# Two attention layers on small graphs: sums over keys by VectorE transposes and row sums, their inverses passed through DRAM

## The chip, the cores and the metric

One Trainium2 chip, one of its cores. The core has TensorE (PE: matmuls, with a weight load ahead of each; PEld), VectorE (DVE), ScalarE (ACT), GpSimd (POOL) and SyncE (SP), which here issues nearly all DMA transfers. Each engine takes its instructions in order, and an instruction may wait for semaphores that other engines or landed transfers raise. The metric is the device time of one execution in microseconds; less is better.

## What is computed

Sixty-four graphs of 256 nodes with 512 features go through two layers, each a LayerNorm, a ReLU, multi-head attention restricted by the graph's adjacency, and a residual sum. Layer 0 has 4 heads of 64 and no self-loops added (a row without neighbours becomes uniform); layer 1 has 8 heads of 64, a gamma and beta, and self-loops. All is fp32.

```python
h = relu(layernorm(x))                        # per node
q, k, v = h @ Wq, h @ Wk, h @ Wv              # split into heads of 64
sim = where(adj, (q @ k.T) / 8, -big)         # per graph and head, 256 x 256
x = x + softmax(sim) @ v @ Wo + bo            # layer 0, 4 heads

h = relu(layernorm(x))
q, k, v = split((h * gamma + beta) @ w_qkv.T)
sim = where(adj | eye, (q @ k.T) / 8, -1e9)
x = x + softmax(sim) @ v @ w_out.T + b_out    # layer 1, 8 heads
```

The softmax's divisor, the sum of the exponentials over the keys, is what the change is about. The kernel holds scores as (keys on partitions) x (queries), so the sum over keys is a sum across partitions.

## The kernel before

**Steps and places.** Two graphs make a step, and there are 32 steps. The program for PE, DVE, ACT and POOL is one list of events, each with a place in time units (`at(period, place, ...)`), sorted by place and emitted in that order; a period is 6.4 units. So for these four engines the order of the work is written by hand. SP's order is not: the framework's scheduler decides in which order SP issues the transfers.

**Heads in pairs.** Two heads (128 columns) make a pair: layer 0 has pairs 0 and 1 (`L0`), layer 1 pairs 0 to 3, taken as `L1A` = (0, 2) and `L1B` = (1, 3).

**Visits.** A period has three visits (`visit`, L1073), each for two pairs: at place 2.0 (here called X: it ends layer 0 of step s+1 and begins `L1A` of step s), at 4.5 (Q: ends `L1A`, begins `L1B`), and at 6.2 (Z: ends `L1B` of s, begins layer 0 of s+2). At its head PE runs, for the two pairs begun at the visit before, `key_sums` (L1007: the sums over keys, four groups of 32 output rows, one for each graph and head, by a matmul with ones) and `weigh` (L976: exponentials times values), and then `scores` for the two new pairs (L920). DVE adds the mask (L944), ACT takes the exponentials (L949), and POOL adds the two halves of the keys into `pd` (`key_halves`, L953), a tile with two buffers.

**Between visits** PE runs sets of seven products (Strassen's scheme, `SET`, `SETC`, `SETC0`), one product taking 1/7 unit: projections to queries and keys (`project_qk`, L803), values (`project_v1`, L844; `project_v0`, L830), output projections (`combine`, L860). The result of each product is moved out of PSUM by DVE or ACT (`evacuate`, `accumulate`), placed at the end of the product. Four PSUM banks (`m0` to `m3`) go round; PE can't write one before its last contents are out. The scheme needs sums of blocks of the activations: `act_sums0` and `act_sums1` (L409 to L414, POOL). After X come the values of step s (set at 2.0), layer 0's output projection of step s+1 (at 3.0, `SETC0`: products 1, 6, 5, 2, 7, 3, 4; product 6 multiplies block 4, which L412 writes) and the second half of the queries and keys (3.5). The output projection is added into `xt`, the residual rows.

**The inverses.** `invert` (L1022) takes reciprocals of the sums, 32 equal rows for each graph and head, from PSUM (L1029), folds an overflow check into `extremes` (L1032), and copies the rows, 32 partitions at a time, with eight transfers a pair (L1041) to all the partitions that hold the head's outputs (`invb`). `normalise` (L1046, POOL) multiplies.

**Other work that the change moves.** For step s+2: `norm0` (statistics, L576/L577), `scale_row` (L592, ACT), `turn_blocks` (L686, DVE transposes of 32x32 blocks) and `move_blocks` (L698, sixteen transfers that complete the transpose of the activations); `neighbours` (L511, DVE: whether a node has a neighbour), `neighbours_out` (L518: writes that to DRAM as `row`, 4 bytes at a time), `neighbours_in` (L523: reads it back to all partitions as `ne`). For step s+1: `load_x` (L493, loads `xt`, at X + 0.1) and `first_bias` (L498, POOL, adds a bias to `xt`, four times, at 2.5, 2.51, 2.85 and 2.86). On POOL the order after X is `key_halves`, `normalise`, `key_halves`, L498 twice, `normalise`, L409 to L414, L498 twice, and then the masks (L560, L563). The finished rows are stored by L894.

Of the kernel before, what the change touches and what calls it, by code (L numbers as in the profile page):

```python
# [315 lines left out]
def fast_path(  # L316
# [63 lines left out]
    ones = const.tile([P, 32], FP, name="ones")  # L380
    nc.vector.memset(ones, 1.0)
# [521 lines left out]
    def scores(s, lyr, pr, second):  # L903
# [32 lines left out]
        pd = sm.tile([P, 2, G, N], FP, name="pd", bufs=2)  # L936
        st["sc", lyr, pr], st["p", lyr, pr] = sc, (p, pd)

    def mask_scores(s, lyr, pr, g):

        st = S[s]
        sc, (p, pd), neg = st["sc", lyr, pr][g], st["p", lyr, pr], st[f"n{lyr}"]
        for e in range(2):
            nc.vector.tensor_tensor(p[e][:, g], sc[e], neg[:, :, g, :], ALU.add)  # L944

    def exponentials(s, lyr, pr, g):
        p, pd = S[s]["p", lyr, pr]
        for e in range(2):
            nc.scalar.activation(p[e][:, g], p[e][:, g], AF.Exp, scale=SCALE)  # L949

    def key_halves(s, lyr, pr, e):
        p, pd = S[s]["p", lyr, pr]
        nc.gpsimd.tensor_tensor(pd[:, e], p[e][:, :, 0, :], p[e][:, :, 1, :], ALU.add)  # L953


    def place_values(s, lyr):
        st = S[s]
        tile_o = act.tile([P, NB, HP1, N], FP, name="oT")
        if lyr:
            st["oT1"] = tile_o  # L960
            st["invb"] = [tile_o[:, 3], tile_o[:, 4]]
            st["inv"] = [tile_o[:, 6, i] for i in range(2)]
        else:
# [3 lines left out]
            st["inv"] = [flat[:, 12 + i] for i in range(2)]  # L967

    def weigh(s, lyr, pr):
        st = S[s]  # L970
        p, _ = st["p", lyr, pr]
# [24 lines left out]
    def key_sums(s, lyr, prs):  # L996

        st = S[s]
        bank = mm_tile([P, 2, N])
        sums_bank[:] = [banks[-1]] if len(prs) > 1 else []  # L1000
        for i, pr in enumerate(prs):
            _, pd = st["p", lyr, pr]
            st["sums", lyr, pr] = bank[:, i]
            for g in range(G):
                for e in range(2):
                    r0 = 32 * (2 * g + e)
                    nc.tensor.matmul(  # L1007
                        bank[r0:r0 + 32, i, :], ones, pd[:, e, g, :], start=True, stop=True,
                        skip_group_check=True,
                    )  # L1010

    def inverse_places(s, lyr, pr, i):

        if (s, lyr) != (NSTEP - 1, 1):
            return S[s]["inv"][i], S[s]["invb"][i]
        if pr == 0:
            invb = wqk0[:, 6].rearrange("p c k o -> p (c k o)").rearrange("p (g n) -> p g n", g=G)
        else:
            invb = act.tile([P, G, N], FP, name="invb", tag=("n0", "ne", "ab")[pr - 1])
        return bo_b[:, i * N:(i + 1) * N], invb  # L1020

    def invert(s, lyr, pr, i, halves=(0, 1)):  # L1022
        st = S[s]
        sums = st["sums", lyr, pr]
        if 0 in halves:
            st["place", lyr, pr] = inverse_places(s, lyr, pr, i)
        inv, invb = st["place", lyr, pr]
        for k in halves:
            nc.vector.reciprocal(inv[:, k * P:(k + 1) * P], sums[:, k * P:(k + 1) * P])  # L1029
        if 1 not in halves:  # L1030
            return
        nc.vector.tensor_tensor_reduce(  # L1032
            out=sums, in0=sums, in1=inv, scale=1.0, scalar=0.0, op0=ALU.add, op1=ALU.max,
            accum_out=extremes[:, units[0]:units[0] + 1],
        )
        units[0] += 1
        for g in range(G):
            for e in range(2):
                r0 = 32 * (2 * g + e)
                for d0 in range(e * DH, (e + 1) * DH, 32):  # L1040
                    nc.sync.dma_start(invb[d0:d0 + 32, g, :], inv[r0:r0 + 32, :])  # L1041
        st["invb", lyr, pr] = invb
# [30 lines left out]
    def visit(period, w, prev, cur):  # L1073
# [4 lines left out]
        if prs:  # L1078
            at(period, w, key_sums, s, lyr, prs)
            if prs[0] == 0 and not last:  # L1080
                at(period, w, place_values, s, lyr)
            for i, pr in enumerate(prs):
                k = i if len(prs) > 1 else pr % 2
                at(period, w + 0.1 * last, invert, s, lyr, pr, k, (0,) if i and not last else (0, 1))
                if not last:
                    at(period, w, weigh_out, s, lyr, pr)
                    at(period, w + (0.55 if len(prs) == 1 else (0.3, 0.75)[i]), normalise, s, lyr, pr)
        for i, pr in enumerate(cur[2]):
# [4 lines left out]
            if i == 1 and len(prs) > 1 and not last:  # L1093
                at(period, w, invert, s, lyr, prs[1], 1, (1,))
# [3 lines left out]
            for e, place in enumerate((0.23, 0.3) if one else ((0.1, 0.11), (0.35, 0.36))[i]):  # L1098
                at(period, w + place, key_halves, *unit, e)

# [24 lines left out]
    visit(-1, 1.54, none, (1, 0, (1,)))  # L1125
    for s in range(NSTEP):
# [6 lines left out]
        for t in range(NT):  # L1133
            at(p, 0.5 + 0.4 * t if s != 1 else 1.95 + 0.1395 * t, norm0, s, t)
            if s == 0:
                at(p, 0.95 + 0.4 * t, first_scale, t)
            else:
                at(p, 2.35 + 0.001 * t if s != 1 else 2.6 + 0.1 * t, scale_row, s, t)
            if not by_tensor(s, 0):
                at(p, (2.45, 2.48, 2.58, 2.6)[t], turn_blocks, s, 0, t)  # L1140
        if not by_tensor(s, 0):
            at(p, 2.61, move_blocks, s)
        for g in range(G):
            at(p, (1.8, 2.7)[s] if s < 2 else 0.7 + 0.14 * g, neighbours, s, g)
# [3 lines left out]
        else:  # L1148
            at(p, 0.9, neighbours_out, s)
            at(p, 1.9, neighbours_in, s)  # L1150
# [104 lines left out]
def kernel(tc, *args):  # L1255
# [3 lines left out]
    with tc.tile_pool(name="guard", bufs=1) as guard:  # L1259
        extremes = guard.tile([P, B // 2 * 6], FP, name="extremes")  # L1260
# [44 lines left out]
```

## Time and profile before

| | |
|---|---|
| runs | 3223.42, 3223.45, 3221.77 us; median 3223.42 |
| profiled execution | 3224.29 us, its span 3222.4 us |
| granted TensorE clock, mean | 0.999 |
| L803, all projections to queries, keys | 1186.4 us busy on PE |
| L860, output projections | 587.9 us |
| L976, exponentials times values | 352.1 us |
| L1029, reciprocals | 376 of 939 ns, 8 of 925 ns |
| L1032, check | 192 of 433 ns, each with a read of 142 ns |
| L686, transposes 128x512 | 240 of 671 ns (median) |
| L511, reductions 128x512 | 64 of 664 ns |
| transfers, median issue to landing | `row` 9.2 us, `ne` 5.1, `xt` 5.8, L1041 1.9, L698 2.0 |

A line of a timeline gives start (us from the span's start), length, engine, line, operation, output and input tile, and how many instructions are merged; brackets at its end give the idle time before it and what ended it. A line of the page's groups gives shapes, the count, then busy time and mean ns of one. SPq is SP's DMA queue; its lines show the issue of a transfer, not its flight. In a table by stretches a column is the engine's busy time with the number of instructions, and the last three are granted clock, DMA share and GB/s.

### The profile page before, as it was taken

Reading aid. Unit: us, or ns where it says so; the run is one execution under the profiler, and the core shown is the slowest. Engines: PE = TensorE matmul, PEld = TensorE weight load, DVE = VectorE, ACT = ScalarE, POOL = GpSimd, SP = SyncE. Lnnn points to the kernel's source line nnn. Section 1 sums busy time; section 2 is a strip of 40 time slices with the busy share of each in tenths; the row PEclk is TensorE's granted clock in tenths of the full one; section 3 lists DMA queues with packets and bytes.
Section 4 is the critical chain, followed back from the end, with each engine's and each line's share of the span. In section 5 each row is a group of like instructions: output and inputs, shape, how many; then the busy total and the mean of one; then the engine's idle time right before and its main releaser. Section 6 shows DMA issues by size and latency. Waiting matters only on the chain.

```text
span 3222.4 us, 59733 instructions
## 1 busy us (share of the span) xinstructions
PE 3196.6 (99%) x22002; PEld 2613.9 (81%) x22002; DVE 2091.9 (65%) x3680; ACT 1256.4 (39%) x2226; POOL 2240.0 (70%) x2124
## 2 busy tenths in 40 slices
PE   8999999999999999999999999999999999999999
PEld 6788888888888888888888888888888888888787
DVE  6656666666666666675666666666666667566655
ACT  4434343343433334343434334343433434343431
POOL 7776776677767767667677667776776766767753
PEclk9999999999999999999999999999999999999999
DMA  4132232232322322223223223232232222322311
GB/s 149 43 86 76 57 86 65 81 82 54 86 69 75 89 61 72 76 70 86 77 56 86 65 81 83 54 85 69 75 88 62 71 76 69 87 77 54 87 30 48
DMA packets 214217, 237.04 MB, mean 74 GB/s; under 512 B 75032, under 2 KB 128416, under 8 KB 213920
## 3 DMA queue, kind: packets, MB, share of 16 engines
q1 hardware_dynamic: 213488, 232.76, 26.4%
q8 instruction: 177, 2.90, 0.4%
q14 instruction: 120, 0.98, 0.2%
q10 hardware_dynamic: 432, 0.40, 0.0%
HBM read 86.12 MB, written 33.62 MB: 37 GB/s over the span
## 4 chain that ended last, share of the span: by engine, by line
PE 93%; DMA 2%; POOL 2%; SPq 1%; issue 1%; DVE 1%; POOLq 0%; DVEq 0%
PE mm L803 36%; PE mm L860 17%; PE mm L844 10%; PE sc L976 10%; PE sc L920 8%; PE mm L830 7%; PE mm L1007 3%; PE mm L920 2%; SPq L1041 1%; DMA xt<-in_x_dram 1%; POOL xt L498 1%; PE mm L886 0%; DMA h<-in_x_dram 0%; DVE oT L1029 0%; PE mm L549 0%
## 5 line engine op out<-in xcount | busy, mean ns | idle before, releaser
L803 PE MATMUL mm<-hT,wqkv 128*128 128x256 f32 x3584 | 787.5, 380 | 0.0
L803 PEld LDWEIGHTS mm<-hT,wqkv 128*128 128x128 f32 x3584 | 678.2, 190 | 102.4 <-issue 11.4
L953 POOL TENSOR_TENSOR pd<-p 128x512 f32<-128x512 f32 x383 | 479.7, 1274 | 298.3 <-ACT p L949 297.6
L860 PE MATMUL mm<-wo,oT 128*128 128x256 f32 x2632 | 587.9, 381 | 9.1 <-POOL oT L412 5.8
L860 PEld LDWEIGHTS mm<-wo,oT 128*128 128x128 f32 x2632 | 498.2, 190 | 89.0 <-issue 7.7
L1029 DVE RECIPROCAL oT<-mm 128x128 f32<-128x128 f32 x376 | 345.3, 939 | 244.3 <-PE mm L1007 239.1
L949 ACT ACTIVATE p<-p 128x512 f32<-128x512 f32 x766 | 439.6, 625 | 137.9 <-DVE p L944 137.9
L944 DVE TENSOR_TENSOR p<-sc,n 128x512 f32<-128x512 f32 x579 | 363.5, 683 | 113.7 <-PE sc L920 112.3
L844 PE MATMUL mm<-wqkv,hT 128*128 128x256 f32 x1792 | 401.9, 382 | 0.0
L803 PE MATMUL mm<-hT,wqk 128*128 128x256 f32 x1792 | 398.9, 382 | 0.8 <-DVE qk L743 0.6
L803 PEld LDWEIGHTS mm<-hT,wqk 128*128 128x128 f32 x1792 | 338.2, 191 | 56.8 <-issue 11.2
L844 PEld LDWEIGHTS mm<-wqkv,hT 128*128 128x128 f32 x1792 | 335.5, 190 | 53.7 <-issue 10.7
L976 PE MATMUL sc<-p,v 128*32 128x256 f32 x6128 | 350.2, 379 | 1.3 <-issue 1.3
L976 PEld LDWEIGHTS sc<-p,v 128*32 128x32 f32 x6128 | 199.8, 110 | 133.3 <-issue 2.3
L988 ACT COPY oT<-sc 128x512 f32<-128x512 f32 x188 | 109.3, 581 | 501.1 <-PE sc L976 495.7
L1046 POOL TENSOR_TENSOR oT<-oT 128x512 f32<-128x512 f32 x188 | 239.9, 1276 | 87.1 <-DMA oT<-oT 79.5
L920 PE MATMUL sc<-qk 64*128 64x256 f32 x2320 | 292.9, 385 | 0.0
L920 PEld LDWEIGHTS sc<-qk 64*128 64x128 f32 x2320 | 218.9, 186 | 58.9 <-issue 39.6
L771 POOL TENSOR_TENSOR xt<-xt,u 128x512 f32<-128x512 f32 x183 | 228.9, 1271 | 3.9 <-DVE xt L760 1.5
L830 PE MATMUL mm<-wv,hT 128*128 128x256 f32 x1024 | 227.0, 379 | 0.4 <-DVE qk L747 0.4
L830 PEld LDWEIGHTS mm<-wv,hT 128*128 128x128 f32 x1024 | 194.3, 190 | 27.2 <-DVE qk L747 0.7
L592 ACT ACTIVATE h<-h,mr,r 128x512 f32<-128x512 f32 x252 | 184.6, 804 | 0.0
(139 smaller groups left out, 3780.4 us busy)
## 6 DMA issues: line engine op xcount, KB each, us to landing
h<-blocks SPq DMA_DIRECT2D x960, 64.0 KB, 2.0
oT<-oT SPq DMA_DIRECT2D x1504, 32.0 KB, 1.9
xt<-in_x_dram SPq DMA_DIRECT2D x31, 1024.0 KB, 5.8
h<-in_x_dram SPq DMA_DIRECT2D x31, 1024.0 KB, 5.4
out_dram<-xt SPq DMA_DIRECT2D x31, 1024.0 KB, 4.6
ne<-row SPq DMA_DIRECT2D x30, 256.0 KB, 5.1
ad<-in_adj_dram SPq DMA_DIRECT2D x32, 128.0 KB, 9.1
wr<-in_L_gnn_w_qkv_dram SPq DMA_DIRECT2D x3, 1024.0 KB, 6.1
```

The lines of the kernel that those rows point to most:

```text
L771: (nc.vector if last else nc.gpsimd).tensor_tensor(r, r, u, ALU.add)
L803: nc.tensor.matmul(bank[:, k, :], w[:, wa, c, k, a * P:(a + 1) * P], st["hT"][:, ba, c, :], start=first and (k, c) == (0, 0), stop=(k, c) ...
L830: nc.tensor.matmul(bank, st["hT"][:, b0 + t // NIC * step, c % HC, i:i + P], wv0[:, c, :], start=(c == 0), stop=(c == NC - 1),)
L844: nc.tensor.matmul(bank[:, t, :], st["hT"][:, ba, c, t * P:(t + 1) * P], wqkv1[:, wa, c, 2, :], start=first and (t, c) == (0, 0), stop=(t, ...
L860: nc.tensor.matmul(bank[:, t, :], oT[:, ba, c, t * P:(t + 1) * P], w[:, wa, c, :], start=first and (t, c) == (0, 0), stop=(t, c) == (NIC - ...
L920: nc.tensor.matmul(sc[g][e][:, kc, :], qk[rows, 1, k0:k0 + P], qk[rows, 0, g * N:(g + 1) * N], start=True, stop=True,)
L944: nc.vector.tensor_tensor(p[e][:, g], sc[e], neg[:, :, g, :], ALU.add)
L949: nc.scalar.activation(p[e][:, g], p[e][:, g], AF.Exp, scale=SCALE)
L953: nc.gpsimd.tensor_tensor(pd[:, e], p[e][:, :, 0, :], p[e][:, :, 1, :], ALU.add)
L976: nc.tensor.matmul(po[r0:r0 + 32, g, :], st[f"v{lyr}"][:, g * NIC + kc, pr * P + r0:pr * P + r0 + 32], p[r0 // DH][:, g, kc, :], start=(kc ...
L1029: nc.vector.reciprocal(inv[:, k * P:(k + 1) * P], sums[:, k * P:(k + 1) * P])
L1046: nc.gpsimd.tensor_tensor(dst, dst, invb, ALU.mult)
```

## The change

The sums over keys no longer run on PE as matmuls with ones. For each pair, DVE transposes `pd` in 32x32 blocks (`turn_keys`: 128x1024) and reduces each block's rows (`key_quarters`: 128x1024 to 128x32); this leaves, for each query, four partial sums, one from each quarter of the partitions. One matmul a visit (`quarters`, a 128x32 matrix of four stacked identities, against `part`, 64 columns for two pairs) adds the four. The result is a 64x32 tile: one reciprocal, one check, one transfer to DRAM (`line`), and from there two transfers a pair that read the 512 values of a head back to its 64 partitions. `pd`, `turned_p`, `part` and `inv` have one buffer each. The transposes and reductions stand one at a time between evacuations; `key_halves` of the second pair move a little later at Q and Z. `norm0`, `scale_row`, `turn_blocks`, `move_blocks`, `neighbours`, `neighbours_out` and `neighbours_in` get new places.

```diff
-    ones = const.tile([P, 32], FP, name="ones")
-    nc.vector.memset(ones, 1.0)
+    quarters = const.tile([P, 32], FP, name="quarters")
+    nc.vector.tensor_tensor(quarters, ident[:, 0:32], ident[:, 32:64], ALU.add)
+    for k in (2, 3):
+        nc.vector.tensor_tensor(quarters, quarters, ident[:, 32 * k:32 * (k + 1)], ALU.add)
...
     def key_halves(s, lyr, pr, e):
-        p, pd = S[s]["p", lyr, pr]
-        nc.gpsimd.tensor_tensor(pd[:, e], p[e][:, :, 0, :], p[e][:, :, 1, :], ALU.add)
+        st = S[s]
+        p = st["p", lyr, pr]
+        if e == 0:
+            st["pd"] = sm.tile([P, 2, G, N], FP, name="pd", bufs=1)
+        nc.gpsimd.tensor_tensor(st["pd"][:, e], p[e][:, :, 0, :], p[e][:, :, 1, :], ALU.add)
+
+    def turn_keys(s):
+        st = S[s]
+        st["turned_p"] = sm.tile([P, 32, 32], FP, name="turned_p", bufs=1)
+        nc.vector.transpose(st["turned_p"], st.pop("pd").rearrange("p e g (b k) -> p (e g b) k", k=32))
+
+    def key_quarters(s, lyr, prs, i):
+        st = S[s]
+        if i == 0:
+            st["part", lyr, prs] = stat.tile([P, 2, 32], FP, name="part", bufs=1)
+        nc.vector.tensor_reduce(
+            st["part", lyr, prs][:, i], st.pop("turned_p"), axis=mybir.AxisListType.X, op=ALU.add
+        )
...
     def key_sums(s, lyr, prs):
...
-            for g in range(G):
-                for e in range(2):
-                    r0 = 32 * (2 * g + e)
-                    nc.tensor.matmul(
-                        bank[r0:r0 + 32, i, :], ones, pd[:, e, g, :], start=True, stop=True,
-                        skip_group_check=True,
-                    )
...
+        part = st.pop(("part", lyr, prs))
+        rows = 32 * len(prs)
+        bank = mm_tile([P, 32])
...
+        sums = bank[:rows]
+        nc.tensor.matmul(
+            sums, part[:, :len(prs)].rearrange("p i b -> p (i b)"), quarters, start=True, stop=True
+        )
+        inv = stat.tile([P, 32], FP, name="inv", bufs=1)[:rows]
+        nc.vector.reciprocal(inv, sums)
         nc.vector.tensor_tensor_reduce(
             out=sums, in0=sums, in1=inv, scale=1.0, scalar=0.0, op0=ALU.add, op1=ALU.max,
-            accum_out=extremes[:, units[0]:units[0] + 1],
+            accum_out=extremes[:rows, units[0]:units[0] + 1],
         )
         units[0] += 1
-        for g in range(G):
-            for e in range(2):
-                r0 = 32 * (2 * g + e)
-                for d0 in range(e * DH, (e + 1) * DH, 32):
-                    nc.sync.dma_start(invb[d0:d0 + 32, g, :], inv[r0:r0 + 32, :])
-        st["invb", lyr, pr] = invb
+        line = dram.tile([len(prs), 2, T], FP, name="line")
+        nc.sync.dma_start(line.rearrange("i e (b q) -> (i e b) q", q=32), inv)
+        for i, pr in enumerate(prs):
+            invb = inverse_place(s, lyr, pr, i if len(prs) > 1 else pr % 2)
             for e in range(2):
+                nc.sync.dma_start(
+                    invb[e * DH:(e + 1) * DH].rearrange("p g n -> p (g n)"),
+                    bass.AP(tensor=line.tensor, offset=line[i, e, 0:1].offset, ap=[[0, DH], [1, T]]),
+                )
+            st["invb", lyr, pr] = invb
...
-            for e, place in enumerate((0.23, 0.3) if one else ((0.1, 0.11), (0.35, 0.36))[i]):
+            for e, place in enumerate((0.23, 0.3) if one else ((0.1, 0.11), (0.495, 0.496) if z else (0.435, 0.436) if q else (0.35, 0.36))[i]):
                 at(period, w + place, key_halves, *unit, e)
+            if cur[:2] == (1, 0):
+                turn, add, key = 0.112, 0.113, (*cur[:2], (0, 1), pr)
+            else:
+                turn, add = (
+                    (0.31, 0.311) if one else ((0.49, 0.491), (0.63, 0.92))[i] if z else
+                    ((0.43, 0.431), (1.02, 1.021))[i] if q else ((0.29, 0.291), (0.43, 0.72))[i]
+                )
+                key = (*cur, i)
+            at(period, w + turn, turn_keys, cur[0])
+            at(period, w + add, key_quarters, *key)
...
-            at(p, 0.5 + 0.4 * t if s != 1 else 1.95 + 0.1395 * t, norm0, s, t)
+            at(p, (0.5 + 0.4 * t, 1.95 + 0.1395 * t)[s] if s < 2 else (0.95, 1.05, 1.2, 1.35)[t], norm0, s, t)
...
-                at(p, 2.35 + 0.001 * t if s != 1 else 2.6 + 0.1 * t, scale_row, s, t)
+                at(p, 1.6 + 0.001 * t if s != 1 else 2.6 + 0.1 * t, scale_row, s, t)
             if not by_tensor(s, 0):
-                at(p, (2.45, 2.48, 2.58, 2.6)[t], turn_blocks, s, 0, t)
+                at(p, AT_X - 0.00035 + 0.00001 * t, turn_blocks, s, 0, t)
         if not by_tensor(s, 0):
-            at(p, 2.61, move_blocks, s)
+            at(p, AT_X - 0.00031, move_blocks, s)
         for g in range(G):
-            at(p, (1.8, 2.7)[s] if s < 2 else 0.7 + 0.14 * g, neighbours, s, g)
+            at(p, (1.8, 2.7)[s] if s < 2 else 1.5 + 0.1 * g, neighbours, s, g)
...
-            at(p, 0.9, neighbours_out, s)
-            at(p, 1.9, neighbours_in, s)
+            at(p, 1.65, neighbours_out, s)
+            at(p, 2.6, neighbours_in, s)
```

## The prediction

> **What bounds the kernel now.** I read the page's busy times, then its chain, then the timeline of one step on TensorE (PE), on the DMA queue (SPq) and on GpSimd (POOL).
>
> ```profile
> PE 3196.6 (99%) x22002; PEld 2613.9 (81%) x22002; DVE 2091.9 (65%) x3680; ACT 1256.4 (39%) x2226; POOL 2240.0 (70%) x2124
> ...
> PE 93%; DMA 2%; POOL 2%; SPq 1%; issue 1%; DVE 1%; POOLq 0%; DVEq 0%
> ...
> L1007 PE MATMUL mm<-pd,ones 128*32 128x256 f32 x1536 | 103.0, 385 | 0.0
> ```
>
> PE is the path: every microsecond taken from it, or put on it as a wait, is a microsecond of the span. The sums over keys (L1007) are on it. One visit:
>
> ```profile
> 1635.31 1.07 PE L1007 MATMUL mm<-pd,ones 128*32 128x256 f32 x16
> 1636.20 3.64 PE L976 MATMUL sc<-p,v 128*32 128x256 f32 x64
> ```
>
> From the first L1007 to the first L976 are 0.89 us. Now the queue of SP and what hangs on it, in the step whose X visit begins at 1596.02 (0.89 us before its first L976, at 1596.91); the next X visit begins at 1695.09.
>
> ```profile
> 1599.05 6.72 SPq L1041 DMA_DIRECT2D oT<-oT  x8
> 1605.82 0.58 SPq L493 DMA_DIRECT2D xt<-in_x_dram  x1
> 1606.50 5.58 SPq L1041 DMA_DIRECT2D oT<-oT  x8
> 1612.74 10.00 SPq L698 DMA_DIRECT2D h<-blocks  x16
> ...
> 1680.96 0.37 SPq L518 DMA_DIRECT2D row<-any_of  x1
> 1681.44 1.91 SPq L485 DMA_DIRECT2D ad<-in_adj_dram  x1
> 1690.05 0.34 SPq L523 DMA_DIRECT2D ne<-row  x1
> ```
>
> ```profile
> 1611.69 2.50 POOL L498 TENSOR_TENSOR xt<-xt,bo_b 128x512 f32<-128x512 f32 x2 [0.56 <-DMA xt<-in_x_dram]
> 1614.15 1.26 POOL L1046 TENSOR_TENSOR oT<-oT 128x512 f32<-128x512 f32 x1
> 1615.37 0.73 POOL L409 TENSOR_TENSOR oT<-oT 128x256 f32<-128x256 f32 x1
> 1616.17 0.72 POOL L412 TENSOR_TENSOR oT<-oT 128x256 f32<-128x256 f32 x1
> ```
>
> ```profile
> 1616.83 6.46 PE L860 MATMUL mm<-wo,oT 128*128 128x256 f32 x28
> ```
>
> This is the stretch that decides. The load of `xt` (L493) is issued at 1605.82, 9.8 us into the visit; GpSimd waits for it by 0.56 us and then does L498 twice, L1046, L409, L412. L412 writes the block that the second product of the layer-0 output projection (L860) multiplies. That product begins four matmuls after 1616.83, at 1617.70; L412 ended at 1616.89. The slack is 0.8 us. SP issues in order: it stood before L523 until the `row` write of 1680.96 had landed (1690.05). Once, early in the span, GpSimd was late:
>
> ```profile
> 128.49 7.32 PE L860 MATMUL mm<-wo,oT 128*128 128x256 f32 x24 [5.51 <-POOL oT L412]
> ```
>
> ```profile
> 123.00:128.40 5.40, 0.00 (x0) 0.00 (x0) 0.00 (x0) 0.58 (x1) 5.40 (x7) 1.00 0.43 102
> 128.40:131.80 3.40, 3.31 (x8) 2.68 (x9) 0.69 (x1) 0.00 (x0) 3.40 (x5) 0.50 0.08 19
> ```
>
> PE stood 5.51 us, and the granted clock (the third figure from the right) was 0.50 for the 3.4 us after it.
>
> **Part 1, PE.** Ninety-five visits with two pairs lose 16 L1007 instructions, 0.888 us from first to next group, and get one fp32 matmul: two instructions with their own weights of 64 columns, 32 columns streamed. No row has that. Below: 0.28 us, two steps of 0.14 (L466: 64 matmuls, each behind a new weight load, 9.2 us). Above: 0.62, twice the 0.31 us that PE takes from the last matmul of one array shape to the first of the next. I take 0.39: a step of 0.16 (0.027 streamed, an eighth of the 0.216 per 256 columns; a load of 0.11 as in L1007; 0.025 from load to matmul), then 0.23 to leave the shape (0.027, the 0.093 by which such a change exceeds 0.216, a load of 0.11). Gain: 95 x (0.888 - 0.39) = 47 us, ends 25 and 58. The two single-pair visits give nothing.
>
> The Trainium skill (TensorE: Matmul & The Clock Gate, LDWEIGHTS) gives columns / 1.2 ns for a weight load, 53 ns for 64 columns; the rows here show 110 ns for 32 columns and 190 for 128. By the page the two loads would cost 0.11 us less a visit and the sum would be 10 us lower.
>
> **Part 2, VectorE.** A visit loses four L1029 at 0.94 and two L1032 pairs at 0.57 (4.9 us). It gets two transposes and two reductions of 128x1024: at most twice L686's 0.67 and twice L511's 0.66, so 5.3; one reciprocal, at most 0.94, and one L1032, at most 0.57. At most 1.9 us more a visit, 181 us against 1130 us of idle VectorE: hidden. The order could expose it. The first transposes stand behind the 2nd evacuation of a set (the 3rd at Q), and the second one waits for GpSimd's `pd`, which now has one buffer and so waits for the first. Walking X and Z (evacuations 0.6 apart, L953 2.5 a pair, 1.74 a product), the 4th VectorE-bound bank of Z comes free just as PE wants it: 0 to 0.2 us, 30 times, at most 6 us. I take 0. If that cover is gone, each late evacuation is PE time one for one.
>
> **Part 3, the inverses.** Reciprocals end about 1 us into a visit rather than 3 to 10. Sixteen DMAs of 0.59 us issue become one write and four reads. For Q and Z this is earlier than needed.
>
> **Part 4, the moved steps.** This is where I put the price. `turn_blocks`/`move_blocks` come forward to the head of the X visit, `neighbours` back to 1.5, `neighbours_out` to 1.65. SP's order is not written by hand, and as built it runs in every step: `row` write, `ad` load, `ne` read, `line` write of X, store, four `line` reads, sixteen moves, and only then the `xt` load. So the 16 moves (all their issues) stand before L493, and the `ne` read, which waits for `row`, before the `line` write. Microseconds from the start of X:
>
> - `row` is issued behind the second L511, which now follows the evacuation L758: that starts 5.08 before X (1690.01 to 1695.09), its successor 0.61 later, L511 takes 0.65. So -3.8. It lands 9.2 later (median of L518): 5.4.
> - `ne` 0.34; the `line` write 1.9 as L1041's landings: 7.65. Farther rows are 1.7 (a store of 128 KB) and 9.2 (`row`).
> - four reads at 0.59 issue, as L1041 (0.34 as L523 below): 10.0.
> - sixteen moves at 0.626 (10.0 by the row above): 20.05. Their transposes are long done.
> - `xt` lands 5.87 later, as 1605.82 to 1611.69: 25.9.
> - L498 twice, L1046, L409, L412, 1611.69 to 1616.89: 5.2, so 31.1.
> - PE wants it at 1617.70 - 1596.02 - 0.50 (part 1) = 21.2.
>
> So PE waits 9.9 us, in the 29 steps whose `xt` load stands there: 288 us. What is late next: after it L498's second pair ends near 35, when PE's next evacuation needs it, and the bias, masks and statistics follow at their old distances. Ends: 8.3 (`row` 8.8, reads 0.34) and 14 (`row` 11.3, a read landing as late as `ne`, 5.1, and holding the moves, which share its semaphores).
>
> The restart is not free: after the one wait of 5.51 us the 24 matmuls took 7.16 us to the next set against 5.22 at 0.2177 each, 1.94 more. 29 x 1.94 = 56 us; ends 0 (clock kept) and 3.4 a time (two such windows).
>
> The Trainium skill (DMA: Bandwidth & Descriptors, Specifications) says that pieces under 512 B cost a read-modify-write; `line` is written in pieces of 128 B. The trace has 9.2 us for pieces of 4 B and 1.9 for 1 KB; were it to cost as `row` does, the sum would be 29 x 7.3 = 212 us higher.
>
> **Sum**, against the profiled run of 3224.3 us (span 3222.4 with 1.9 around it; median of the runs 3223.4): 3224.3 - 47 + 288 + 56 = 3521.
>
> **Rivals.**
> - *The wait for `row` is not in the way* (it lands sooner, or the statistics run earlier). Then `line` lands at 0.9 + 1.9 = 2.8, reads to 5.2, moves to 15.2, `xt` at 21.1, L412 at 26.3: 5.1 us a step. 3224.3 - 47 + 148 + 56 = 3381. For it: only one DMA decides. Against: SP's waits list 243 us before L523 for `row`, 29 times.
> - *Faster: the `xt` chain is off the path.* It decides at `xt` landed by 16.0 (21.2 - 5.2). Then only part 1 counts: 3224.3 - 47 = 3177. For it: PE is 99% busy, the removal is real. Against: ten microseconds of moves now stand before the load that had 0.8 us of slack.
> - *VectorE's new order holds PE as well*, 1 us at X and Z each: 29 x 2 = 58, so 3579. For it: the transpose waits for GpSimd with evacuations behind it. Against: at X the larger wait swallows it, and VectorE idles a third of the time.
>
> **How the numbers follow.** Forecast 0.72, first rival 0.16, second 0.05, third 0.07. The forecast's own ends: 3224.3 - 58 + 29 x 8.3 = 3407 and 3224.3 - 25 + 29 x (14 + 3.4) = 3704; all bad ends together are unlikely, so I stop at 3640, and go down to 3370 for the first rival. 0.2% (6.4 us) is about what this measurement tells from no change: faster 0.05, within it 0.01, slower 0.94.
>
> **What would show it.** PE idle before L860's later products (in the changed file `combine`), released by GpSimd's activation sums, some 10 us a step; GpSimd idle before the first bias for `xt`; SP waiting for `row` across the start of X; granted clock 0.5 in short windows after each wait; from the first key-sum matmul to the first weighting matmul 0.4 us, not 0.89. I am wrong if `xt` lands by 16 us after the start of X, or if the output projection waits for nothing.

## The result, and the profile after

The changed kernel takes 3622.93 us (median of 4 runs, 3621.27 to 3624.66), the kernel before 3222.68 us beside it: a ratio of 1.1242, 95% interval [1.1223, 1.1262]. It is 400 us slower. The forecast was 3521 us within 3370 to 3640. The profiled execution took 3621.27 us, its span 3619.4.

From the page of the changed kernel: busy times, the chain by engine, and two groups.

```profile
PE 3240.9 (90%) x20660; PEld 2640.5 (73%) x20660; DVE 2152.5 (59%) x3590; ACT 1253.7 (35%) x2226; POOL 2237.7 (62%) x2124
...
PE 73%; DMA 8%; issue 7%; POOL 6%; SPq 3%; DVE 1%; ACT 0%; another core or an unknown queue 0%; POOLq 0%; DVEq 0%; ACTq 0%
...
L501 POOL TENSOR_TENSOR xt<-xt,bo_b 128x512 f32<-128x512 f32 x124 | 153.9, 1263 | 304.4 <-DMA xt<-in_x_dram 304.4
```

PE has 1342 instructions fewer (22,002 - 1536 + 194 = 20,660), and yet is busy 44.3 us longer; and it stands for 3619.4 - 3240.9 = 378.5 us, where it stood for 25.8 us before. GpSimd's bias (L501, before L498) waited 304 us for `xt`. What PE waited for, from its view of waits (total, times, longest, in us):

```profile
PE mm L863 <- POOL oT L415: 315.7, 30, 12.0
PE mm L847 <- DVE v L746: 22.9, 22, 2.3
PE sc L923 <- ACT oT L1006: 12.9, 7, 3.4
```

The first line is the wait that was forecast: product 6 of layer 0's output projection (L863, before L860) for the activation sum of block 4 (L415, before L412). One step, from the timelines. The X visit begins at 1795.22.

PE:

```profile
1795.22 0.30 PE L1022 MATMUL mm<-quarters,part 128*64 128x32 f32 x2
1795.45 3.66 PE L994 MATMUL sc<-p,v 128*32 128x256 f32 x64
...
1828.36 8.13 PE L863 MATMUL mm<-wo,oT 128*128 128x256 f32 x24 [10.81 <-POOL oT L415]
```

SP's queue:

```profile
1791.46 0.37 SPq L521 DMA_DIRECT2D row<-any_of  x1
1791.87 0.51 SPq L488 DMA_DIRECT2D ad<-in_adj_dram  x1
1800.93 0.34 SPq L526 DMA_DIRECT2D ne<-row  x1
1801.37 0.48 SPq L1033 DMA_DIRECT2D line<-inv  x1
1801.95 0.53 SPq L897 DMA_DIRECT2D out_dram<-xt  x1
1805.16 2.37 SPq L1037 DMA_DIRECT2D oT<-line  x4
1807.63 10.05 SPq L701 DMA_DIRECT2D h<-blocks  x16
1817.72 0.58 SPq L496 DMA_DIRECT2D xt<-in_x_dram  x1
```

GpSimd:

```profile
1809.05 1.28 POOL L1053 TENSOR_TENSOR oT<-oT 128x512 f32<-128x512 f32 x1 [3.71 <-DMA oT<-line]
...
1823.12 2.48 POOL L501 TENSOR_TENSOR xt<-xt,bo_b 128x512 f32<-128x512 f32 x2 [10.34 <-DMA xt<-in_x_dram]
...
1827.58 0.72 POOL L415 TENSOR_TENSOR oT<-oT 128x256 f32<-128x256 f32 x1
```

Read from SP: the `ne` read is issued only at 1800.93, when the `row` write of 1791.46 has landed; behind it stand `line`, four reads, sixteen moves, and last the load of `xt`, 22.5 us into the visit (9.8 before the change). It lands at 1823.12; L415 ends at 1828.30, and PE goes on at 1828.36. Had the load of `xt` landed 10.8 us sooner, that line of PE would carry no bracket.

The table by stretches (start:end and length, then busy us of PE, PEld, DVE, ACT, POOL, then granted clock, DMA share, GB/s) shows the clock around this wait. PE stops at 1817.55; the clock is halved from 1819.66, in the midst of the wait, until 1833.31, 4.95 us after PE goes on:

```profile
1816.24:1819.65 3.41, 1.31 (x7) 0.80 (x5) 0.81 (x2) 0.58 (x1) 0.00 (x0) 1.00 0.47 108
1819.66:1823.07 3.41, 0.00 (x0) 0.00 (x0) 0.00 (x0) 0.00 (x0) 0.00 (x0) 0.50 0.73 276
1828.36:1833.31 4.95, 4.95 (x12) 3.96 (x13) 1.38 (x2) 0.00 (x0) 4.79 (x5) 0.50 0.00 0
1833.32:1836.70 3.38, 3.37 (x16) 2.69 (x15) 2.25 (x4) 0.00 (x0) 3.38 (x3) 1.00 0.02 5
```

The account of the span, +397 us. The 22.9 us at L847 belong to the stall: that wait comes earlier in the same set, and PE goes on behind product 6 when L415 ends, however long it stood before.

| term | forecast | found | how |
|---|---|---|---|
| sums off PE | -47 | -62.5 | 95 x (0.888 - 0.23); 0.23 from 1795.22 to 1795.45 |
| stall behind X | +288 | +332.8 | 315.7 + 22.9 - 5.8 before; 30 steps of 11.3 |
| clock | +56 | +106.8 | PE busy +44.3, less the -62.5 |
| PE's other waits | 0 | +19.9 | idle +352.7 (378.5 - 25.8) less 332.8 |
| sum | +297 | +397.0 | |

### The profile page after: what moved, and what is told of

It reads as the page before. It is cut to its first block, busy times and chain, and to the rows that moved or that the text cites. A ratio compares the mean times of both kernels' runs of the same rounds, so it can differ in the third digit from the quotient of the medians.

```text
span 3619.4 us, 54427 instructions
## 1 busy us (share of the span) xinstructions
PE 3240.9 (90%) x20660; PEld 2640.5 (73%) x20660; DVE 2152.5 (59%) x3590; ACT 1253.7 (35%) x2226; POOL 2237.7 (62%) x2124
## 4 chain that ended last, share of the span: by engine, by line
PE 73%; DMA 8%; issue 7%; POOL 6%; SPq 3%; DVE 1%; ACT 0%; another core or an unknown queue 0%; POOLq 0%; DVEq 0%; ACTq 0%
PE mm L806 32%; PE mm L863 15%; PE sc L994 8%; PE sc L923 6%; PE mm L833 6%; SPq L701 3%; DMA row<-any_of 2%; PE mm L847 2%; DMA line<-inv 2%; PE mm L923 2%; POOL xt L501 2%; DMA xt<-in_x_dram 2%; DMA oT<-line 2%; POOL pd L958 2%; POOL oT L1053 1%
## 5 line engine op out<-in xcount | busy, mean ns | idle before, releaser
L863 PE MATMUL mm<-wo,oT 128*128 128x256 f32 x2632 | 669.2, 415 | 316.3 <-POOL oT L415 315.7
L863 PEld LDWEIGHTS mm<-wo,oT 128*128 128x128 f32 x2632 | 548.1, 211 | 428.7 <-POOL oT L415 328.9
L847 PE MATMUL mm<-wqkv,hT 128*128 128x256 f32 x1792 | 410.8, 385 | 23.1 <-DVE v L746 22.9
L847 PEld LDWEIGHTS mm<-wqkv,hT 128*128 128x128 f32 x1792 | 334.6, 191 | 85.6 <-DVE v L746 32.9
L501 POOL TENSOR_TENSOR xt<-xt,bo_b 128x512 f32<-128x512 f32 x124 | 153.9, 1263 | 304.4 <-DMA xt<-in_x_dram 304.4
L923 PE MATMUL sc<-qk 64*128 64x256 f32 x2320 | 309.3, 389 | 13.5 <-ACT oT L1006 12.9
L964 DVE STREAM_TRANSPOSE turned_p<-pd 128x1024 f32<-128x1024 f32 x192 | 237.4, 1237 | 109.6 <-POOL pd L958 109.6
L923 PEld LDWEIGHTS sc<-qk 64*128 64x128 f32 x2320 | 228.3, 188 | 77.8 <-issue 40.6
L761 DVE TENSOR_TENSOR u<-mm,u 128x512 f32<-128x512 f32 x62 | 42.8, 691 | 401.3 <-PE mm L863 401.3
L994 PEld LDWEIGHTS sc<-p,v 128*32 128x32 f32 x6128 | 190.3, 110 | 118.2 <-issue 0.3
L740 ACT COPY qk<-mm 128x512 f32<-128x512 f32 x96 | 55.6, 579 | 601.6 <-PE mm L806 598.2
L971 DVE TENSOR_REDUCE part<-turned_p 128x32 f32<-128x1024 f32 x192 | 232.8, 1213 | 4.4
```

Source lines behind the costliest of these rows:

```text
L847: nc.tensor.matmul(bank[:, t, :], st["hT"][:, ba, c, t * P:(t + 1) * P], wqkv1[:, wa, c, 2, :], start=first and (t, c) == (0, 0), stop=(t, ...
L863: nc.tensor.matmul(bank[:, t, :], oT[:, ba, c, t * P:(t + 1) * P], w[:, wa, c, :], start=first and (t, c) == (0, 0), stop=(t, c) == (NIC - ...
L923: nc.tensor.matmul(sc[g][e][:, kc, :], qk[rows, 1, k0:k0 + P], qk[rows, 0, g * N:(g + 1) * N], start=True, stop=True,)
L964: nc.vector.transpose(st["turned_p"], st.pop("pd").rearrange("p e g (b k) -> p (e g b) k", k=32))
L971: nc.vector.tensor_reduce(st["part", lyr, prs][:, i], st.pop("turned_p"), axis=mybir.AxisListType.X, op=ALU.add)
L994: nc.tensor.matmul(po[r0:r0 + 32, g, :], st[f"v{lyr}"][:, g * NIC + kc, pr * P + r0:pr * P + r0 + 32], p[r0 // DH][:, g, kc, :], start=(kc ...
```

## The experiments

In what follows "clock" is the same reckoning for each run: PE's busy time less 3134.1 us (3196.6 - 62.5), which is what PE's work takes at the clock of the kernel before (0.999).

**1. The moves behind the load.**

```diff
-            at(p, AT_X - 0.00031, move_blocks, s)
+            at(p, 2.61, move_blocks, s)
```

> The changed kernel with the sixteen moves placed at 2.61 again, so that SP issues the xt load before them; all else, the VectorE transposes and reductions too, as changed. Theory (PE waits for the chain moves, xt load, first bias, activation sums): xt is issued 10 us earlier in each step, PE's 10.5 us wait before product 6 of layer 0's output projection falls under 2 us, and the half-clock windows go with it: 3200 to 3260 us. Rival (VectorE's new instructions hold the evacuations and with them PE): nothing changes, 3600 or more.

Measured: 3420.68 us, ratio 1.0613 [1.0592, 1.0634]. This is neither expectation: the direction was the theory's, the size was not, and 200 us of the 400 come back. The stall falls from 315.7 to 88.9 us (28 times), but SP still waits for `row` ahead of `line`, so `xt` goes out some 14 us into the visit (median 13.7), and a second wait appears:

```profile
PE mm L863 <- POOL oT L415: 88.9, 28, 5.1
PE mm L847 <- DVE v L746: 50.1, 26, 3.2
```

The path of the second is that of GpSimd's line at 1809.05 above: GpSimd's normalisation waits for the late inverses with the second `pd` behind it, VectorE's transpose waits for that `pd`, and the evacuation L746 stands behind the transpose. The clock's loss is 99 us, nearly that of the changed kernel, though the waits are less than half as long (160 against 351 us).

**2. The `ne` read off SP's queue.**

```diff
-        nc.sync.dma_start(ne, bass.AP(tensor=row.tensor
+        nc.scalar.dma_start(ne, bass.AP(tensor=row.tensor
```

> The changed kernel with only the read of the neighbour row (ne) issued by ACT's queue instead of SP's, so that SP no longer stands before the line write until the row write has landed; the moves stay ahead of the xt load. Theory: line goes out about 5 us earlier in each step and PE's wait shrinks from 10.5 to 6 or 7 us: 3470 to 3510 us. Rival (the row wait is hidden anyway): 3610 to 3630.

Measured: 3563.37 us, ratio 1.1056: 59 us gained, about half of the least that the theory expected (113). SP no longer waits for `row`, and `line` is issued 1.1 us into the visit, but its readers don't come sooner in proportion. From the issue of `line` at X to the issue of its first read are 7.1 us (median of 25 steps), against 4.6 in the changed kernel.

**3. Both.**

> Both edits: moves at 2.61 and ne read on ACT's queue. Theory: xt lands by 14 us after the start of X, PE waits for nothing there, and only the gain of the PE part is left (0.66 us a visit in the changed kernel's trace, 62 us): 3155 to 3185 us, faster than the kernel before. Rival (VectorE's new order costs PE something of its own): above 3223.

Measured: 3307.16 us, ratio 1.027 [1.0251, 1.029]. A miss by 120 us. The time lies in the rival's range, but not by its mechanism: PE waits 1.3 us in all for the evacuation L746, and the largest wait is still that for L415. SP's queue at one X visit, which begins at 1646.75:

```profile
1642.99 0.37 SPq L521 DMA_DIRECT2D row<-any_of  x1
1643.41 0.51 SPq L488 DMA_DIRECT2D ad<-in_adj_dram  x1
1647.83 0.48 SPq L1033 DMA_DIRECT2D line<-inv  x1
1648.94 0.38 SPq L897 DMA_DIRECT2D out_dram<-xt  x1
1655.22 2.37 SPq L1037 DMA_DIRECT2D oT<-line  x4
1657.69 0.53 SPq L496 DMA_DIRECT2D xt<-in_x_dram  x1
```

Nothing on SP stands in front of `line`, and still its first reader comes 7.4 us behind it, 12.2 us behind `row`. So the `row` write seems to cost twice: the wait of SP, and, with that gone, a late landing of `line` (runs 6 and 12 test this). PE still waits 55.9 us for L415 and 20.2 for L1006 on ScalarE, and the clock loses 54.

**4. The new sums alone.** All seven moved steps (statistics, scaling, transposes, moves, and the three of the neighbours) back at their old places; only the sums are new.

> The new sums over keys with every moved step (norm0, scale_row, turn_blocks, move_blocks, neighbours, neighbours_out, neighbours_in) at its old place. Theory: SP has the xt load ahead of the moves and the row write has landed before X, so PE doesn't wait for xt: 3155 to 3230 us; the spread is for VectorE, which has its four block transposes of the X visit beside the new ones and may evacuate late. Rival (the new sums themselves, by VectorE or by the way through DRAM, make the loss): 3400 or more.

Measured: 3261.92 us, ratio 1.0122 [1.0105, 1.0139]: 1.2% slower than before, 32 us above the theory's range and far below the rival's. `line` lands in 1.7 us here (median; `row` is down before X), and the stall at product 6 is one wait of 4.1 us. What is left is VectorE:

```profile
PE mm L847 <- DVE v L746: 45.8, 30, 2.8
PE mm L806 <- DVE qk L746: 31.5, 30, 1.1
```

At X, the four transposes of the activations (2.45 us) stand between the second transpose of the sums and the evacuation L746; after Z, statistics and a neighbours' reduction do. PE gains 62.5 us, stands 80 longer than before (106.0 against 25.8) and loses 20 by its clock: the span is 37 us longer. So the sums do need some steps moved: VectorE's new work does not fit in between as they stood.

**5. The places alone.** The kernel before, with its matmuls of ones and its copies of inverses, and the seven steps at the changed places.

> The kernel before, with its matmuls of ones and its copies of the inverses, and only the moved steps at the changed places (statistics, scaling, transposes and moves ahead of X, neighbours later). Theory (the places, not the new sums, make the loss): SP has the sixteen moves ahead of the xt load here too, and the neighbours' row as late, so the output projection waits about as long a step as in the changed kernel or longer (the sixteen copies of inverses stand around it): 3500 to 3850. Rival (the loss needs the new sums, whose line write is what the row write holds): 3220 to 3300.

Measured: 3862.55 us, ratio 1.1979, 12 us above the expected range. PE waits 339.5 us for block 4's sum and 159.2 for a normalisation. The places by themselves cost 640 us; the new sums, whose five transfers a visit replace sixteen, win back 240 of them. The loss is mainly that of the places; the sums alone cost 39 us (run 4).

**6. The row early.** The changed kernel with the moves at 2.61 and the neighbour steps at their old places; the other moves stay.

```diff
-            at(p, AT_X - 0.00031, move_blocks, s)
+            at(p, 2.61, move_blocks, s)
-            at(p, (1.8, 2.7)[s] if s < 2 else 1.5 + 0.1 * g, neighbours, s, g)
+            at(p, (1.8, 2.7)[s] if s < 2 else 0.7 + 0.14 * g, neighbours, s, g)
-            at(p, 1.65, neighbours_out, s)
-            at(p, 2.6, neighbours_in, s)
+            at(p, 0.9, neighbours_out, s)
+            at(p, 1.9, neighbours_in, s)
```

> The changed kernel with the sixteen moves back at 2.61 (behind the xt load) and the neighbour steps back at their old places (row write at 0.9, read at 1.9), everything else as changed. In the first experiments the line write, issued while the row write was in flight, reached its readers 7.4 us later, and in the run with all moved steps at their old places 3.0 us later. Theory (the row write's flight holds the line write behind it, whoever waits): row has landed before X, the four reads are issued about 3 us after the line write, the xt load by X + 7, the output projection waits for nothing; time 3165 to 3200. Rival (the line write is slow for another reason, such as its 128 B pieces): line to first read stays 7 us, and the output projection keeps about 2 us a step; 3240 to 3300. Second rival: the neighbours' reductions at 0.7 and 0.84 again stand before an evacuation after Z, as in the run of the sums alone: 31 us more, about 3210.

Measured: 3216.49 us, ratio 0.9978 [0.9968, 0.9988]. It is 0.2% below the kernel before, above the range of the theory, and near the second rival's 3210. From `line` to its first read at X are 1.9 us (median) with `row` down; the stall is 7.8 us. What remains, in PE's waits:

```profile
PE mm L863 <- DVE xt L763: 19.1, 30, 0.7
PE mm L806 <- DVE qk L746: 9.4, 30, 1.3
PE mm L863 <- POOL oT L415: 7.8, 8, 5.8
```

The second rival, the reduction ahead of the evacuation after Z, is the second line. The first line is GpSimd's second bias, late because GpSimd waits with the second `pd` for the transpose of the first (one buffer; 1.94 us in the step at 432 us).

**7. The row early and nothing else.** As 6, with the moves where the change put them: the prediction's first rival, built.

> The changed kernel with only the neighbour steps back at their old places, so that the row write has landed before X, and the sixteen moves still ahead of the xt load. It is the first rival of the prediction made real (the wait for row is not in the way). Theory (moves ahead of the load, and the row's flight, each cost by themselves and add up on one chain): line at X + 0.9, reads 4 to 6.4, moves to 16.5, xt issued there, landed at 22.4, the sums of block 4 at 27.6 to 28.5 against 22.2 wanted, so 5.4 to 6.3 us a step and the clock's loss: 3380 to 3450. Rival (only one of them binds; the moves alone make the whole wait): 3560 to 3625. Second rival (the row alone makes it): 3215 to 3280.

Measured: 3464.19 us, ratio 1.0747 [1.0725, 1.0768], 14 us above the expected range.

```profile
PE mm L863 <- POOL oT L415: 205.9, 30, 8.3
```

The wait is 6.9 us a step and the clock loses 86. The two causes lie one behind the other on one chain: taking the row away gives 159 us, the moves 202, both 406.

**8. The transposes early.** As 6, with the first transpose of the sums ahead of the evacuation that it stood behind, and the neighbours' reductions behind theirs.

```diff
-                    (0.31, 0.311) if one else ((0.49, 0.491), (0.63, 0.92))[i] if z else
-                    ((0.43, 0.431), (1.02, 1.021))[i] if q else ((0.29, 0.291), (0.43, 0.72))[i]
+                    (0.31, 0.311) if one else ((0.4, 0.491), (0.63, 0.92))[i] if z else
+                    ((0.43, 0.431), (1.02, 1.021))[i] if q else ((0.2, 0.291), (0.43, 0.72))[i]
-            at(p, (1.8, 2.7)[s] if s < 2 else 0.7 + 0.14 * g, neighbours, s, g)
+            at(p, (1.8, 2.7)[s] if s < 2 else 0.73 + 0.14 * g, neighbours, s, g)
```

> The kernel of the run with the early row, with three places more: the first transpose of the exponentials' sums stands ahead of the second product's evacuation instead of behind it, at X (0.20 after the visit) and at Z (0.40), so that the single buffer of pd is free 1.9 us earlier for GpSimd, and the neighbours' reductions go to 0.73 and 0.87, behind the evacuation at 0.714 instead of ahead of it. In the run with the early row TensorE still waited 19 us (30 times) for the accumulation into xt, which stood behind GpSimd's late bias, 9.4 us (30 times) for the evacuation after Z, 7.8 us (8 times) for the activation sums, and its clock was 0.997. Theory (these are all late for the one buffer of pd and for the neighbours): all three go and the clock's share with them; 3165 to 3185, so the new sums give nearly the 62 us that they take from TensorE. Rival (VectorE's row of work is merely late in another place, the transpose ahead of the evacuation holding a bank): waits stay at 20 us or more, 3190 to 3225.

Measured: 3188.07 us, ratio 0.9889 [0.9873, 0.9906], 3 us above the theory's range and 2 below the rival's. The wait after Z is gone (9.4 to 1.4 us), the wait for `xt` falls from 19.1 to 7.8 (13 times). Where it is left, `xt` is late: its median flight is 7.4 us (5.8 to 8.8 with the moves right behind it), against 5.8 before the change, and not the 9 that the expectation of run 9 gives.

**9. The last block transpose later,** so that the moves don't follow the load at once.

```diff
-                at(p, AT_X - 0.00035 + 0.00001 * t, turn_blocks, s, 0, t)
+                at(p, AT_X - 0.00035 + 0.00001 * t if t < 3 else 2.44, turn_blocks, s, 0, t)
```

> The kernel with the early transposes, and the last of the four block transposes of the activations put at 2.44, behind the second transpose of the sums, so that the sixteen moves are issued some 10 us later. In the run with the early transposes the xt load was issued at X + 7 but took 9 us to land rather than the 5.4 to 5.9 it takes alone, since the moves are issued right behind it. Theory (the moves share the DMA engines with the load and delay it): xt lands 3 us earlier, GpSimd's bias follows at once, TensorE's last 14 us of waits at the output projection go with their clock; 3165 to 3182. Rival (the load is slow for another reason, or VectorE's later transpose holds an evacuation): 3183 to 3200.

Measured: 3177.66 us, ratio 0.9851 [0.9834, 0.9867]. The moves are now issued 8 to 10 us behind the load. `xt` flies 6.0 us (median of 20 landings): ten take 5.2 to 5.4 us, ten 6.5 to 7.5, and what holds those ten is not shown. GpSimd's wait for it falls from 22.8 us (16 times) to 2.0 (twice). This version beats both kernels, by 46 us the one before (1.5%). Its PE is busy 3143.7 us of 3176.1 and has one wait left in the steps' stretch at product 6 (4.3 us).

**10 and 11. A second write that nobody reads.** The kernel of 6 with `any_of` written once more, right behind `row`, in 512 pieces of 4 B (run 10) and in 128 pieces of 16 B (run 11).

```diff
+    def row_again(s):
+        again = dram.tile([NT, P], FP, name="again")
+        nc.sync.dma_start(again.rearrange("t p -> p t"), S[s]["any"])
...
+            at(p, 1.65, row_again, s)
```

> The kernel of the run with the early row, with a second write of the same 512 values to a DRAM tile that nothing reads, in pieces of 4 B like the first, issued right behind it some 12 us before X. Nobody waits for it. Theory (such a write takes some 9 us in flight, one after the other, and holds the next small write behind it): it lands about 6 us after the start of X, the line write issued at X + 1 reaches its readers 6 to 8 us later rather than 2 to 4, the xt load goes out at X + 10 or 11, and the time is that of the run with both moves late and the read on ScalarE's queue, 3270 to 3330. Rival (the line write is not held by a write that nobody waits for): 3210 to 3230, the same as without it.

> The same second write of the same 512 values, but in 128 pieces of 16 B (the four values of a partition together, in another order, to a tile that nothing reads). Theory (the number of small pieces makes the flight long, not the bytes): a quarter of the pieces, some 2 to 3 us behind the first write, landed before X; line to first read 2 to 4 us, time 3210 to 3235. Rival (any small write of this kind holds the next as long): as the run with the second write in 4 B pieces.

Measured: 3217.66 and 3217.73 us, the time of 6. The theory that such writes take 9 us each, one after the other, is wrong. The second write of 4 B pieces landed 10.6 us (median) after an issue 0.4 us behind `row`, which took 9.4: 1.6 us after it, well before X. So these runs don't tell whether a write in flight holds `line`; that was a badly placed test. Run 11's time lies in the range of its theory, but its write took 9.0 us and landed just behind `row`, so it doesn't tell what 128 pieces cost by themselves. The two runs do show something else. The landings of the second write in 16 B pieces, and of the adjacency load issued next:

```profile
DMA to landing us min/median/max: 8.5/9.0/11.9
```

```profile
DMA to landing us min/median/max: 2.2/8.6/11.5
```

The load can land in 2.2 us; behind `row` it takes 8.6 (median). What was issued behind `row` on its queue landed no sooner than `row`.

**12. The row write on another queue.** The kernel of 3, with `row` too issued by ScalarE.

```diff
-        nc.sync.dma_start(S[s]["row"].rearrange("t p -> p t"), S[s]["any"])
+        nc.scalar.dma_start(S[s]["row"].rearrange("t p -> p t"), S[s]["any"])
```

> The kernel of the run with both moves late and the read on ScalarE's queue (3307 us), with the row write, too, issued by ScalarE, behind its scalings of h (some 1.5 us later than SP issued it). Nothing else changes. In the runs before, a write in 16 B pieces and the adjacency load, both issued on SP's queue right behind the row write, landed with it, about 9 us after their issue, though the adjacency load takes 2.2 us at the least; and the line write's readers came 3 us after the row had landed. Theory (SP's queue takes its transfers in order, and what is issued behind the row write waits for it there): with the row on another queue the line write lands after 1.7 us, the first read is issued 2 to 3.5 us behind it, the adjacency load's median landing falls to 2 to 5 us, the output projection's wait of 56 us goes, and the time is 3205 to 3250. Rival (the hold is in the DMA engines or in DRAM, which all queues share): line to first read stays 6 to 9 us, time 3300 to 3340.

Measured: 3281.53 us (two runs, 3272.62 and 3290.43), ratio 1.0181 [1.0114, 1.0248]: between the two expectations by time, and the two runs differ by 18 us. The mechanism is the rival's: from `line` to its first read at X are 6.1 us (median of 27 steps; 7.1 in run 3, 1.9 with `row` down). One visit, SP's queue, which has no `row` on it; ScalarE's queue issued that at 1629.55:

```profile
1634.39 0.48 SPq L1033 DMA_DIRECT2D line<-inv  x1
1635.50 0.39 SPq L897 DMA_DIRECT2D out_dram<-xt  x1
1641.19 2.36 SPq L1037 DMA_DIRECT2D oT<-line  x4
```

If `row` takes 9.4 us as elsewhere, it lands at 1639.0, and the reads come 2.2 us later. The hold is not in SP's queue.

The trace's records of DMA packets and of semaphore updates say more. In this visit all 528 packets of ScalarE's queue (the 512 pieces of `row` and 16 more) had started by 1631.72, but the updates of its semaphore came from 1635.96 to 1639.41. In 17 of 29 X visits all 64 packets of `line` had started 1.4 us after its issue, as in run 6 with `row` down (18 of 29); yet the last update of its semaphore came 4.4 to 7.5 us after the issue here, 1.7 to 3.2 us in run 6. So in these visits what came late was the signal of the landing, not the sending of the packets.

The gain (26 us by the medians, 34 by the profiled spans) comes with a stall of 49.3 instead of 55.9 us, 10.4 instead of 20.2 for L1006, and 20 less of clock. The adjacency load had all its packets started 2.0 us after its issue (on SP's queue behind `row`, in run 6, 7.2 us or more), but the last update of its semaphore came after 6.6 us (median of 27), not the 2 to 5 of the theory.

## Why the prediction was right, and where its sizes were off

**The mechanism was right.** Order on SP, the wait for `row` ahead of `line`, sixteen moves ahead of `xt`, GpSimd's sums late, PE standing at product 6: each step stands in the timelines above, and runs 1, 5, 6 and 7 take it apart. The time was 102 us above the forecast, of a loss of 400, and near the upper end of the range; three costs were put too low, by 45, 51 and 20 us, and a gain 15 us larger than forecast hid a part of it. Forecast and measurement of the chain, from the start of X in the step shown: `row` issued -3.8 and -3.8; `ne` 5.4 and 5.7; reads begin 7.65 and 9.9; moves end 20.05 and 22.5; `xt` landed 25.9 and 27.9; block 4's sum 31.1 and 33.1.

**The two microseconds** are one step's: "the `line` write 1.9 as L1041's landings". It took 3.8 there (1801.37 to 1805.16). Alone it takes 1.7 us (runs 4, 6 to 11), so the row chosen was right for the write and wrong for the place: it flies beside the `ne` read, the adjacency load and the store, and its packets start 3.2 us after its issue (median), against 1.1 at Q and Z. PE's want, at 22.3, holds the 0.86 us that it had waited for L746. So the stall is 11.3 us a step on the mean, not 9.9, in 30 steps, not 29: 45 us in sum.

The Trainium skill (DMA: Bandwidth & Descriptors, Specifications) says that transfers under 512 B are read-modify-writes. The prediction priced the case that `line`, in pieces of 128 B, costs as much as `row`; 1.7 against 9.4 us says that it doesn't.

**Part 1 was too careful.** A visit's sums take 0.23 us, not 0.39: 62.5 us gained, above the upper end of 58. The step "then 0.23 to leave the shape" failed; there is no such cost visible behind the second instruction. The weight load of 64 columns takes 133 ns, so the 53 ns of the skill's rule (TensorE: Matmul & The Clock Gate, LDWEIGHTS) aren't reached either, and that the gain by the rule, 57, would have been nearer to the truth is luck.

**The clock was the largest error:** 107 us instead of 56, above its own end of 99. One restart before the change (7.32 us for 24 matmuls after 5.51 us of waiting) was taken for all. In the changed kernel the 30 such restarts take 7.2 to 8.7 us, median 8.1, against some 5.4 without a wait: about 79 us of the 107. The other waits drop the clock too.

**The third rival's mechanism is there, its price is not.** PE waits at X for L746 (22.9 us), but as the prediction said, the larger wait swallows it; after Z it waits 1.3 us in all. That it is there at all comes from the late inverses, by way of GpSimd (run 1). By itself VectorE's new order costs 77 us (run 4), where the old places are kept: the change's new places for the transposes and the neighbours do serve the sums, and it is the moves and `row` behind them that cost. PE's other waits, +20 us, are mostly those for L1006 (12.9), which the prediction did not name. What ScalarE waits for there, the trace doesn't show; where `row` lands before X (runs 6 to 9), one such wait of 3.4 us is left, early in the span, so it seems to hang on the late `row`.

**The first rival,** 3381, was built in run 7 and came out at 3464: the stall was 206 us, not 148, and the clock 86, not 56, while part 1 gave 16 more; 9 of the rest is the wait after Z. Its mechanism is real, its sizes have the forecast's errors.

**The second rival,** 3177, is the time of run 9, 3177.66. By mechanism it is that rival, with other places than the changed kernel has: the chain is off the path. That the numbers meet is luck: the rival has a gain of 47 us and no other term; run 9's span is 46 us shorter, the 62.5 us of part 1 less 10 in the clock and 7 in PE's waits.

## What to carry to other kernels

Before moving a step, list all that it issues on a queue with an order of its own, and look for the load behind it that has the least slack: here sixteen cheap moves went ahead of one load with 0.8 us to spare, and a write of 2 KB in 4 B pieces went from where nobody saw its 9 us to where everybody did. When such a chain is late for two reasons, taking one away shows only part of the gain. Price a wait of TensorE by its length and by the slow matmuls after it: run 1 lost nearly as much clock (99 us) behind 160 us of waits as the changed kernel (107 us) behind 351.

## What the runs showed of the hardware that was not expected

**A write in small pieces holds back the landing of what is issued after it, on other queues too.** With `row` in flight, `line` took 6.1 to 7.1 us to its readers instead of 1.9, whether SP or ScalarE had issued `row`, and the adjacency load 8.6 instead of 2.2. The Trainium skill (DMA: Bandwidth & Descriptors, Queues, rings and completion order) states that the write which raises a transfer's semaphore lands only after every earlier write of that DMA engine, across its queues, and that ScalarE's and SP's transfers run on the same 16 engines. Runs 10 to 12 agree with it, and in most X visits of run 12 only the signal was late, by the packet records. Behind `row` on its own queue (run 6) a part of the adjacency load's packets was late as well. It is not shown why 512 pieces need 9.4 us when 512 more need only 1.6 on top.

**The clock drops after short waits.** At product 6, in the changed kernel and runs 1 to 3, 6 to 8 and 12, the matmuls after the 40 waits of up to 1.87 us all ran at full speed (20 in 4.58 us), those after 29 of the 36 waits from 1.88 to 3.8 us were slowed (24 in 7.1 us or more, 5.4 at full speed), and those after every longer one. So a wait of 2 us can cost more in clock than in length. The Trainium skill (TensorE: Matmul & The Clock Gate, The HAM clock gate) gives about 3.4 us without work until the clock is halved, in windows that run on regardless of the kernel. The traces agree with the windows, but not with a whole one without work. In each of the 14 traces all changes of the clock lie on one grid of 3.41 us. Of 250 changes to half (those of the first 20 us left out), 239 follow a window in which PE stood for 2.0 us or more; of 12,676 windows after which the clock stayed full, one does. The clock came back only after windows in which PE worked for 2.76 us or more. So a wait of 2 to 4 us halves the clock or not as it lies in the grid: in the table above PE stood for 2.1 us of the window that ends at 1819.65.

**A load is slowed by the moves issued behind it.** `xt` (1 MB) landed after 8.3 us (median, run 6; 7.4 in run 8) with sixteen moves of 64 KB right behind it, and after 6.0 us with the moves 8 to 10 us behind it (run 9).
